# Polynomial convolution and attention in one launch: the first image in seven chunks of 448 pixels, its way out behind the next chunk's products, and scores copied with turned sign and a running minimum

## The chip, the cores and the metric

The kernel runs on one core of one Trainium2 chip. A core has TensorE (PE, matrix products; its weight loads are shown as PEld), VectorE (DVE), ScalarE (ACT), GpSimd (POOL) and SyncE (SP), which run side by side, each through its own list of instructions in order, and wait for each other by semaphores. SBUF is the on-chip memory of 128 partitions; PSUM holds what PE writes. DMAs are issued here by SP and, in the opening, by ACT.

The metric is the device time of one launch in microseconds (us). Before the change the median of three runs is 5033.5 us (5032.83 to 5038.3).

## What is computed

32 images of 64 channels and 56 x 56 pixels (3136) go through two layers, all in float32. Layer 0 multiplies channels of a group with each other, in pairs and triples, and takes weighted sums of these products. Layer 1 is attention of every pixel over every pixel, with a double softmax, then a 3x3 convolution per channel.

```python
# layer 0: 8 groups of 8 channels
p2 = x[:, :, _I2] * x[:, :, _J2]
y2 = jnp.einsum('bgihw,goi->bgohw', p2, W2).reshape(B, Ch, H, Wd) + b2[None, :, None, None]
p3 = x[:, :, _I3] * x[:, :, _J3] * x[:, :, _K3]
y3 = jnp.einsum('bgihw,goi->bgohw', p3, W3).reshape(B, Ch, H, Wd) + b3[None, :, None, None]
return inp + y2 * beta2 + y3 * beta3 * CONV3_SCALE
# layer 1
g = jnp.clip(_bn(conv1x1(l, w_inside), gamma1, beta1, mean1, var1), 0.0, 6.0)
theta = l[:, :c_red]                       # 32 of the 64 channels
f = jnp.einsum('niab,nicd->nabcd', theta, theta)
f = jax.nn.softmax(f.reshape(n, h * w, h, w), axis=1)
f = jax.nn.softmax(f.reshape(n, h * w, h * w), axis=2)
out = jnp.einsum('nabcd,nicd->niab', f.reshape(n, h, w, h, w), g) / h * w
out = depthwise_conv3x3(out, w_dw)
return _bn(out, gamma2, beta2, mean2, var2) + l
```

The products of the pixels' scores are symmetric, so the first softmax (over the key's axis) can be taken along rows of a tile of scores, and the second along the other axis by normalising sums.

## The kernel before

**Images and tiles.** Images are taken in pairs, 16 pairs, which share the 128 partitions of `y` (three buffers, `ys`). For each image the 3136 x 3136 scores are made in tiles of 128 pixels by 3136; a pair has 49 tiles (the two remainders of 64 pixels share one), 784 in all. Tile t goes through `scores` (PE writes half a tile of 1568 columns into the four banks `ps`, DVE copies it into `e`, twice), `first_softmax`, `second_softmax` (one exponential each on ACT, in place), and three tiles later (`LAG`) through `attend`, where PE multiplies it with g into the banks `av` and `ax`. The banks of `ps` exist once: the second half's scores wait for the first half's copy. There are four buffers of `e`.

**The statistics of a tile.** Each copy is a multiplication by 1.0 with a running maximum, whose result goes into one of two columns of `mx`. `first_softmax` takes the negative of the larger one with a `tensor_reduce` into `nm` (line 512 and following), and the exponential uses it as bias with scale 1.0. `second_softmax` takes the reciprocal `rz` of the sum `z`.

**Layer 0.** `x` lies in memory so that a tile of 128 partitions and w pixels of "0", "a", "2", "4" or "b" holds the channels rotated by some offset, once for each half k of an image's channels. `products` makes, for each k, the product q = x0 * xa, then p = q * x for "0", "2", "4" and "b", and p4 from the two tiles "c". `poly` multiplies rounds of these with weights on PE into a bank, and `poly_out` adds bias and input into `y` on DVE. A chunk has 242 pixels (`PCH`, 13 chunks, `PCS`), because in the steady stage its sum shares the bank `ax` with attention. Loads stand in a list `plan`; `prefetch` issues from it while a slot of the kind is free (`XB`: 7, 13 and 3 slots) and `credit` lasts, and `products` frees slots. Product buffers are counted by `ROOM` and `taken`.

**The order of the work.** Every engine's instructions are pinned to the order in which the program writes them (`Pinned`), DMAs too. Each DMA adds to one of eight counters, and one that takes up a counter waits until the earlier DMA on it has landed. The image that the first tiles need (image 0 of pair 0, channel halves `ONE`) is made ahead of the tile loop, under the key -1: `feed(0, c, ONE, dve)` puts all 13 chunks on the list, its loads alternately on SP and ACT and its products on DVE. `first_poly(c)` runs the 12 matmuls of chunk c, taking up products as they come, and then its `poly_out`; `first_g(c - 1)` follows with g for the pixels then ready: `g_in` on PE, `g_out` and `prepare` on DVE. After the last chunk `load_theta(0)` copies channels of `y` into four groups of partitions of `th` with four DMAs on SP, and the last g follows.

ACT's list begins with 15 loads of weights and constants, then the two square roots of the batch norms, then its share of the image's loads. DVE's list has the scaling of weights and the batch norms' constants ahead of the first product.

**The tile loop.** In each step t: `run(t, "loads")`, `run(t, "feed")`, a `pace` that renews `credit`, scores of half 0, attention of tile t - 3, units of layer 0 or of g (`aux0`, `aux1`), scores of half 1, and the exponentials. Image 1 of pair 0 (`TWO`) is put on the list at t = 0, its products made on POOL, its sums spread over the first tiles; the following pairs are made the same way, all four channel halves at once, in the tiles of the pair before.

Of the kernel before, what the change touches and what calls it, by code (L numbers as in the profile page):

```python
# [12 lines left out]
AX = mybir.AxisListType  # L13
# [57 lines left out]
def tile_poly_conv_attention(  # L71
# [123 lines left out]

    b3row = const.tile([128, C], FP, name="b3row")
# [13 lines left out]
    dve.tensor_tensor(bias0, bias0, t0, ALU.add)  # L210

# [9 lines left out]
    for k in range(GM):  # L221
# [13 lines left out]
    yt = yp.tile([128, 3, N], FP, name="y")  # L235
    ys = [yt[:, p, :] for p in range(3)]
    pool.memset(ys[0][C:, :], 0.0)
# [4 lines left out]

    LOADS = {
        "0": [(0, 1, 0, 0)],
        "a": [(0, 1, 0, 1)],
        "2": [(0, 1, 2, 0)],
        "4": [(0, 1, 4, 0)],
        "b": [(0, 2, 5, 0), (1, 2, 1, 0)],  # L250
    }
# [11 lines left out]
    def start(out, in_, queue=sync):  # L263
        credit[0] -= 1
        queue.dma_start(out=out, in_=in_)

    def load_next():
        tag, key = plan.pop(0)
        n, c, ks, name, k, queue = key
# [3 lines left out]
        if name == "c":  # L273
            t = xp.tile([128, 2, PCH], FP, name=f"xc_{ident}", tag=tag, bufs=XB[tag])
            at = slice(ks[0] * 32, ks[-1] * 32 + 32)
            for d in range(2):
                src = bass.AP(
                    x.tensor,
                    ((4 * n + ks[0]) * EXT + 4 * d) * 4 * N + p0,
                    [[EXT * 4 * N, len(ks)], [N, 32], [1, w]],  # L280
                )
                start(t[at, d, :w], src, queue)
            loaded[key[:-1]] = [t[at, d, :w] for d in range(2)]
            return
        t = xp.tile([128, PCH], FP, name=f"x{name}_{ident}", tag=tag, bufs=XB[tag])
        for s0, every, d, grow in LOADS[name]:
# [5 lines left out]
            start(t[s0::every, :w] if every > 1 else t[:, :w], src, queue)  # L292
        loaded[key[:-1]] = t[:, :w]
# [9 lines left out]
    def products(n, c, ks, eng):  # L303
# [16 lines left out]
        for k in ks:  # L320
# [4 lines left out]
            eng.tensor_tensor(q, x0[k], xa, ALU.mult)  # L325
# [3 lines left out]
        for r, of in enumerate(("0", "2", "4", "b")):  # L329
            rounds.append({})  # L330
            yield "pr", len(ks)
            for k in ks:
# [4 lines left out]
                eng.tensor_tensor(p, rounds[0][k], xr, ALU.mult)  # L337
# [8 lines left out]
        eng.tensor_tensor(p4, both[0], both[1], ALU.mult)  # L346
# [27 lines left out]
    def feed(n, c, ks, eng):  # L374
# [3 lines left out]
        for tag, name, k in todo:  # L378

            queue = act if eng is dve and len(plan) % 2 else sync  # L380
            plan.append((tag, (n, c, ks, name, k, queue)))
        feeds.append((products(n, c, ks, eng), None))
# [12 lines left out]
    def poly(n, c, ks, rs, acc=None):  # L395

# [3 lines left out]
        own = acc is not None  # L402
        if not own:
            acc = ax[:, AUX:]
        at = slice(ks[0] * 32, ks[-1] * 32 + 32)
        for r in rs:
            for k in ks:
                pe.matmul(
                    out=acc[k * 32 : k * 32 + 32, :w],
                    lhsT=wq[:, r, k % 2, :] if r < NRND else w4[at, k * 32 : k * 32 + 32],  # L410
                    rhs=rounds[r][k],
                    start=own and r == 0,
# [5 lines left out]
    def poly_out(n, c, ks, acc=None):  # L418

        if acc is None:  # L420
            acc = ax[:, AUX:]
# [6 lines left out]
            ys[n % 3][at, p0 : p0 + w], acc[at, :w], bias0[at], xc, ALU.add, ALU.add  # L428
# [5 lines left out]
    def load_theta(b):  # L434
        y = ys[b // 2 % 3]
        p0 = (b % 2) * C
        th = thp.tile([128, N], FP, name=f"th_{b}", tag=f"th{b % 2}")
        for r in range(4):
            start(th[r * 32 : r * 32 + 32, :], y[p0 : p0 + CRED, :])
        ths[b] = th  # L440
# [36 lines left out]
    def scores(t, half):  # L477
        n, kind, q = tile_at(t)
        if half == 0:
            es[t] = ep.tile([128, N], FP, name=f"e_{t}", tag="e")  # L480
            mx = sp.tile([128, 2], FP, name=f"mx_{t}", tag="mx")
            nm = sp.tile([128, 1], FP, name=f"nm_{t}", tag="nm")
            z = sp.tile([128, 1], FP, name=f"z_{t}", tag="z")
            rz = sp.tile([128, 1], FP, name=f"rz_{t}", tag="rz")
            stats[t] = mx, nm, z, rz
        p = ps.tile([128, HALF, BANK], FP, name=f"ps_{t}_{half}", tag="ps")
        for j in range(HALF):
# [12 lines left out]
        e = es[t][:, half * HALF * CH : (half + 1) * HALF * CH]  # L500
        dve.tensor_scalar(
            e.rearrange("p (j c) -> p j c", c=CH), p[:, :, :CH], 1.0, None, ALU.mult, ALU.max,
            accum_out=stats[t][0][:, half : half + 1],
        )

    def first_softmax(t):
        mx, nm, z, _ = stats[t]
        dve.tensor_reduce(nm, mx, AX.X, ALU.max, negate=True)
        act.activation(es[t], es[t], AF.Exp, bias=nm, scale=1.0, accum_out=z)

    def second_softmax(t):
        _, _, z, rz = stats.pop(t)
# [178 lines left out]
    put(-1, "aux0", lambda: [feed(0, c, ONE, dve) for c in range(NPC)])  # L691
    put(-1, "aux0", lambda: prepare(FOR_G))
    banks = {}

# [241 lines left out]
```

## Time and profile before

| What | Value |
|---|---|
| median of three runs | 5033.5 us |
| the profiled execution, whole | 5033.6 us |
| its span | 5031.8 us |
| granted PE clock, mean | 0.983 |
| start of the first copy of scores / first exponential | 146.92 us / 152.55 us |
| POOL's first product of image 1 | 146.20 us |
| exponentials, two for each tile | 2912 and 2896 ns |
| copy of half a tile of scores | 1790 ns |

The span is the time from the first to the last instruction of the profiled execution; the run's time has 1.8 us around it. Times within a profile count from the span's start. A row of instructions names the line, the engine and the operation, what it writes and reads, its shapes and count, the busy time and mean duration, and the idle time of the engine just before it with what ended that. All instructions pass through one helper, so they carry its line, L109, and are told apart by the tiles' names. The chain of waits is followed back from the last instruction to what released each step.

### The profile page before, as it was taken

What the parts mean: (1) busy time and instruction counts of PE and PEld (TensorE: products, weight loads), DVE (VectorE), ACT (ScalarE), POOL (GpSimd) and SP (SyncE); (2) the same over time, 40 slices, a digit from 0 to 9 for tenths busy, and PEclk for the clock granted to TensorE, in tenths of its full rate; (3) what the DMA queues carried; (4) which work ended last, traced back from release to release, by engine and by line L of the source; (5) the groups of instructions that cost most, each with busy time, mean ns of one, the idle gap of its engine ahead of it and who ended that gap; (6) DMA issues with size and microseconds to landing.
All of it is one profiled execution on the core that took longest, in us unless ns stands there. A gap on an engine that the chain in (4) does not pass through costs nothing.

```text
span 5031.8 us, 240733 instructions
## 1 busy us (share of the span) xinstructions
PE 4753.8 (94%) x105924; PEld 3340.6 (66%) x105924; DVE 4222.6 (84%) x6962; ACT 4545.5 (90%) x2356; POOL 3194.2 (63%) x4325
## 2 busy tenths in 40 slices
PE   3898999999999999999999999999999999999995
PEld 1465676776767677676766767676676767667663
DVE  4465698898989889898988989898898989889887
ACT  0577899999999999999999999999999999999995
POOL 0667585876858587585857758586775858677000
PEclk7899999999999999999999999999999999999998
DMA  5555656555565555655565565556556555654201
GB/s 144 140 153 152 150 147 149 145 146 143 143 147 144 147 142 144 145 147 139 152 149 137 142 148 148 139 149 149 143 137 145 151 142 145 151 139 120 44 10 33
DMA packets 892956, 684.17 MB, mean 136 GB/s; under 512 B 291584, under 2 KB 877568, under 8 KB 887808
## 3 DMA queue, kind: packets, MB, share of 16 engines
q1 hardware_dynamic: 879368, 659.52, 51.4%
q8 instruction: 828, 13.57, 1.1%
q10 hardware_dynamic: 12536, 9.25, 0.7%
q14 instruction: 224, 1.84, 0.1%
HBM read 565.65 MB, written 25.69 MB: 118 GB/s over the span
## 4 chain that ended last, share of the span: by engine, by line
PE 71%; DVE 21%; DMA 4%; issue 2%; POOL 1%; SPq 1%; ACT 0%; ACTq 0%; POOLq 0%; DVEq 0%
PE av L109 30%; PE ps L109 24%; PE ax L109 16%; DVE e L109 15%; DVE y L109 3%; DMA xc_None<-in_x_dram 2%; DVE num L109 1%; DMA xa<-in_x_dram 1%; SPq L109 1%; POOL p L109 1%; DMA x<-in_x_dram 1%; DVE rd L109 0%; DVE nm L109 0%; POOL q L109 0%; DMA xb<-in_x_dram 0%
## 5 line engine op out<-in xcount | busy, mean ns | idle before, releaser
L109 DVE TENSOR_SCALAR_CACHE_REDUCE e<-ps 128x1568 f32<-128x1568 f32 x1568 | 2806.6, 1790 | 508.1 <-PE ps L109 462.9
L109 PEld LDWEIGHTS av<-gq,e 128*64 128x64 f32 x64512 | 2014.1, 138 | 864.7 <-issue 806.7
L109 ACT ACTIVATE e<-e,nm 128x3136 f32<-128x3136 f32 x784 | 2282.8, 2912 | 310.8 <-DVE rz L109 228.3
L109 POOL TENSOR_TENSOR p<-q,x 128x242 f32<-128x242 f32 (+1 forms) x2418 | 1781.1, 769 | 939.6 <-PE ax L109 843.0
L109 ACT ACTIVATE e<-e,rz 128x3136 f32<-128x3136 f32 x784 | 2270.3, 2896 | 0.0
L109 PE MATMUL av<-gq,e 128*64 128x65 f32 x64512 | 2227.2, 225 | 3.9 <-ACT e L109 3.2
L109 PE MATMUL ps<-th 32*128 32x392 f32 (+1 forms) x12800 | 1489.4, 541 | 109.7 <-DVE e L109 96.7
L109 PEld LDWEIGHTS ps<-th 32*128 32x128 f32 (+1 forms) x12800 | 491.3, 181 | 448.0 <-DVE e L109 368.4
L109 DVE SCALAR_TENSOR_TENSOR y<-tt,wdt,y 128x605 f32<-128x605 f32 (+4 forms) x720 | 742.4, 1032 | 6.7 <-DMA tt<-tr 5.3
L109 POOL TENSOR_TENSOR p<-q,xb 128x242 f32<-128x242 f32 x806 | 592.5, 762 | 230.6 <-PE ax L109 218.1
L109 POOL TENSOR_TENSOR q<-x,xa 128x242 f32<-128x242 f32 x806 | 561.5, 722 | 216.0 <-DMA xa<-in_x_dram 208.2
L109 PE MATMUL ax<-gq,e 128*64 128x65 f32 x12288 | 489.7, 222 | 0.0
L109 PE MATMUL ax<-p,wq 128*32 128x242 f32 (+1 forms) x6448 | 481.5, 373 | 1.5
L109 PEld LDWEIGHTS ax<-gq,e 128*64 128x64 f32 x12288 | 425.3, 138 | 0.0
L109 POOL TENSOR_SCALAR y<-y,bias 128x616 f32<-128x616 f32 (+1 forms) x80 | 162.8, 2036 | 147.5 <-PE ax L109 137.7
L109 PEld LDWEIGHTS ax<-p,wq 128*32 128x32 f32 x6448 | 178.9, 109 | 111.4 <-POOL p L109 18.8
L109 DVE SCALAR_TENSOR_TENSOR y<-ax,bias,xc_None 128x242 f32<-128x242 f32 (+3 forms) x208 | 97.1, 467 | 108.8 <-PE ax L109 103.1
L109 POOL TENSOR_TENSOR p<-xc_None 128x242 f32<-128x242 f32 (+3 forms) x208 | 127.6, 614 | 78.8 <-DMA xc_None<-in_x_dram 68.6
L109 PE MATMUL ax<-wit,y 128*64 128x64 f32 x3136 | 143.8, 223 | 18.6 <-DVE ax L109 9.6
L109 PE MATMUL ax<-p,w 128*32 128x242 f32 (+1 forms) x1612 | 123.9, 369 | 31.6 <-POOL p L109 31.6
L109 ACT ACTIVATION_READ_ACCUMULATOR e<-e,nm 128x1 f32 x784 | 145.6, 186 | 0.0
L109 DVE TENSOR_REDUCE nm<-mx 128x1 f32<-128x2 f32 x784 | 121.7, 155 | 27.2
(73 smaller groups left out, 1368.1 us busy)
## 6 DMA issues: line engine op xcount, KB each, us to landing
x<-in_x_dram SPq DMA_DIRECT2D x2268, 121.0 KB
xb<-in_x_dram SPq DMA_DIRECT2D x1512, 60.5 KB
xa<-in_x_dram SPq DMA_DIRECT2D x756, 121.0 KB
th<-y SPq DMA_DIRECT2D x128, 392.0 KB
xc_None<-in_x_dram SPq DMA_DIRECT2D x360, 121.0 KB
x<-in_x_dram SPq DMA_DIRECT2D x190, 116.0 KB
out_dram<-y SPq DMA_DIRECT2D x64, 308.0 KB
tt<-tr SPq DMA_DIRECT2D x128, 100.0 KB
```

What stands on the lines that cost most here:

```text
L109: i = f(*args, **kw)
```

## The change

Two parts are changed.

**The first image.** The 13 chunks of 242 pixels become seven of 448 (`FW`, `FCS`), each with a PSUM bank of its own: the four banks of `ps` and the three of `av`, which nobody else uses yet. Loads go into slots of 448 columns of the four buffers of `e` (28 slots, 12 for a chunk), products into slots of `ys[1]`, `ys[2]` and `tt` (21 slots, 10 for a chunk; p4 is written over its second input). Loads alternate between SP and ACT one by one. The loads of chunks 0 and 1 and the products of chunk 0 are written ahead of the scaling of weights; products of chunk 1 and loads of chunk 2 after it, ahead of the batch norms. Then for each chunk c: the matmuls of c, the sum of c - 1, the loads of c + 2, the products of c + 1, and g of c - 1. At c = 5 the first five chunks of theta are copied (2240 columns), and image 1's loads are put on the list, 12 of them issued at once; the other 896 columns follow after the last sum. Products of layer 0 in the tile loop stay on POOL, loads there on SP.

**The scores.** The copy multiplies by -1.0 and keeps a running minimum. The first half's minimum goes to column 0 of `nm`; the second half's copy takes that column as its second scalar, one value for each partition, and leaves the minimum of both in column 1. The `tensor_reduce` is gone, and the exponential has scale -1.0 and that column as bias.

```diff
+    FW = N // 7
+    FCS = [(p, FW) for p in range(0, N, FW)]
+    firsts = [ep.tile([128, N], FP, name=f"first_{i}", tag="e") for i in range(4)]
+    fx, fp = parts(firsts), parts(ys[1:] + [tt])
...
+    def first_loads(c):
+        p0, w = FCS[c]
+        def load(dst, k, d, grow, steps):
...
+            (act if fat["q"] % 2 else sync).dma_start(out=dst, in_=src)
+            fat["q"] += 1
...
+    def first_products(c):
+        xs = fxs[c]
...
+        q = {k: product(xs["0", k], xs["a", k]) for k in (0, 1)}
+        frs[c] = [q] + [{k: product(q[k], xs[a, k]) for k in (0, 1)} for a in "024b"]
+        dve.tensor_tensor(xs["c", 1], xs["c", 0], xs["c", 1], ALU.mult)
+        frs[c].append(dict.fromkeys((0, 1), xs["c", 1]))
+    first_loads(0)
+    first_loads(1)
+    first_products(0)
     b3row = const.tile([128, C], FP, name="b3row")
...
     dve.tensor_tensor(bias0, bias0, t0, ALU.add)
+    first_products(1)
+    first_loads(2)
     s1 = rsqrt_eps("bn1", row("var1"), C)
...
-            mx = sp.tile([128, 2], FP, name=f"mx_{t}", tag="mx")
-            nm = sp.tile([128, 1], FP, name=f"nm_{t}", tag="nm")
+            nm = sp.tile([128, 2], FP, name=f"nm_{t}", tag="nm")
...
         dve.tensor_scalar(
-            e.rearrange("p (j c) -> p j c", c=CH), p[:, :, :CH], 1.0, None, ALU.mult, ALU.max,
-            accum_out=stats[t][0][:, half : half + 1],
+            e.rearrange("p (j c) -> p j c", c=CH),
+            p[:, :, :CH],
+            -1.0,
+            nm[:, :1] if half else None,
+            ALU.mult,
+            ALU.min,
+            accum_out=nm[:, half : half + 1],
         )
     def first_softmax(t):
-        mx, nm, z, _ = stats[t]
-        dve.tensor_reduce(nm, mx, AX.X, ALU.max, negate=True)
-        act.activation(es[t], es[t], AF.Exp, bias=nm, scale=1.0, accum_out=z)
+        nm, z, _ = stats[t]
+        act.activation(es[t], es[t], AF.Exp, bias=nm[:, 1:], scale=-1.0, accum_out=z)
...
+    prepare(FOR_G)
+    NF = len(FCS)
+    first_poly(0)
+    for c in range(1, NF):
+        first_poly(c)
+        first_out(c - 1)
+        if c + 2 < NF:
+            first_loads(c + 2)
+        if c + 1 < NF:
+            first_products(c + 1)
+        if c == 5:
+            load_theta(0, 0, FCS[5][0])
+            for b in range(NPC):
+                feed(0, b, TWO)
+            credit[0] = 12
+            advance()
+        first_g(c - 1)
+    first_out(NF - 1)
+    load_theta(0, FCS[5][0], N)
+    first_g(NF - 1)
```

## The prediction

> **What bounds the kernel now.** I read the page's first two parts, then stretches of time one by one, because the two edits lie in different stages: one in the opening, one in every tile of scores.
>
> ```profile
> span 5031.8 us, 240733 instructions
> PE 4753.8 (94%) x105924; PEld 3340.6 (66%) x105924; DVE 4222.6 (84%) x6962; ACT 4545.5 (90%) x2356; POOL 3194.2 (63%) x4325
> ```
>
> The 94% is a mean. By stretches (columns: stretch, length, busy us and instructions of PE, PEld, DVE, ACT, POOL, then granted clock, DMA share, GB/s):
>
> ```profile
> 20.00:40.00 20.00, 5.33 (x24) 2.15 (x22) 10.63 (x31) 0.00 (x0) 0.00 (x0) 0.67 0.70 188
> 80.00:100.00 20.00, 8.94 (x72) 4.33 (x72) 11.23 (x34) 0.00 (x0) 0.00 (x0) 0.67 0.57 158
> 180.00:200.00 20.00, 16.82 (x288) 9.91 (x280) 9.14 (x16) 11.61 (x6) 15.01 (x24) 1.00 0.52 142
> 1000.00:1400.00 400.00, 395.07 (x9036) 281.32 (x9030) 355.79 (x578) 383.65 (x199) 288.07 (x388) 1.00 0.55 142
> ```
>
> There are three stages. In the **opening** (to the first exponential at 152.55) no engine is over 60% busy, and DMA is at 0.57 to 0.70. In the **second stage** (to some 280 us) POOL makes image 1's products beside the first tiles. In the **steady stage** PE is 98.8% busy. What sets the pace of the opening is in the chain of waits (start, us, what):
>
> ```profile
> 52.72 0.53 SPq L109
> 53.31 0.61 SPq L109
> 53.97 0.60 SPq L109
> 54.62 5.19 DMA xa<-in_x_dram
> 60.48 0.41 DVE p L109
> ```
>
> Three issues at 0.6 us, a landing of 5.19 us, one product, then again: a loop of latency. Buffers come free only as DVE consumes, and each load also waits until an earlier one has landed on its counter (eight, shared by the SP and ACT queues). A chunk's sum leaves PSUM at 52.24 and at 122.89, eight chunks apart: 8.8 us for 242 pixels. The last sum is at 134.76, theta is issued from 135.24, and its four parts reach PE at 139.28, 141.12, 143.10 and 145.21.
>
> In the second stage the chain repeats every 9.3 us: p4 products of POOL end a wait for the xc load at 156.15, 164.92, 174.31, 184.62 and so on to 241.21. In the steady stage the chain has two faces: PE alone (av, ax, ps), and where attention is light, a ring:
>
> ```profile
> 2612.98 1.81 DVE e L109 x2
> 2614.83 0.98 PE ps L109 x8
> 2615.84 1.81 DVE e L109 x2
> 2617.69 1.06 PE ps L109 x8
> ```
>
> There is one set of score banks, so scores wait for the copy and the copy for scores, 2.86 us a half. "DVE e" is 15.1% of the whole chain: 760 us / 1.81 = 420 of 1568 copies.
>
> **The opening, part by part.** Pixels and bytes stay: 7 chunks of eight loads of 229 KB, four of 115 and four of 57 make 2.52 MB a chunk, 17.7 MB in all. Issues fall from 13 x 14 = 182 to 7 x 16 = 112, on two queues at 0.6 us: 4.8 us a chunk, not a bound. Costs of a chunk of 448:
> - DVE: a 128x242 product takes 405 ns alone, six in a row 2.01 us, 335 each, so 83 beyond 242/0.96 ns. For 448: 467 + 83 = 550 ns, eleven make 6.05 us. With the sum (0.68) and one or two groups of g (0.4 to 0.7 each) 7.3 us.
> - DMA: 188 GB/s at a share of 0.70 is 268 at full share. I take 274, as packets are twice as long (1792 B; no row shows them): 9.2 us. The ends are 13.4 us (188 GB/s, the best 20 us seen) and DVE's 7.3 us.
> - PE: a chunk of 242 took 5.20 us in the chain at 123.40 and 2.65 at 129.43 (two chunks in 5.29). Times 448/242: 9.6 and 4.9 us.
>
> Two rules are weighed here. The Trainium skill ("DMA: Bandwidth & Descriptors", Bandwidth) says to batch transfers to a MiB, and that those under 64 KB are descriptor-dominated. Its table (0.95 us for 64 KB, 6.15 for 1 MB) gives about 1.84, 1.23 and 0.9 us for the three sizes, 23 us a chunk taken singly: 161 us, no gain at all. The row speaks otherwise: 121 KB would by that table take 1.26 us, 96 GB/s, and 20 to 40 us moved 188, so transfers overlap; I go by the row. The other ("TensorE: Matmul & The Clock Gate", Part 1) has PE at half clock until a window of about 3.4 us was busy. The rows agree (0.67; 5.20 against 2.65). By the cold price PE needs 9.6 us a chunk and ties with DMA; by the warm one it is hidden. Products now come in runs of 6 us, so I take mostly warm.
>
> The order written out: sum of c-1, loads of c+2, products of c+1, g of c-1. The sum has poly of c-1 finished a whole product run earlier, so PE's tail is covered by products; if PE is cold throughout that cover is gone, about 1 us a chunk. Loads have two chunks of lead, 15 us against a landing of 5, so latency is covered and only the rate remains.
>
> The times: ACT's queue holds the weight loads until 11.2 us, and SP's fourth load waits on a counter of theirs, as SP did here until 10.26. So from 12 us, with 0.69 MB already moved: chunks 0, 1, 2 land at 20.6, 29.8, 39.0. New wait: the square roots of batch norm now stand behind the ACT half of chunk 2's loads, to 35; DVE's chain behind them (13.46 to 18.68 here) ends at 41, and sum 0, products 2 and chunk 3's loads stand behind it. Sum 0 at 41.7, products 2 end 47.8, products 3 at 55.1, products 4 at 62.4. From there landing leads: chunk 5 lands 69.6, chunk 6 at 78.8. At chunk 5 SP also issues the first theta part (4 x 287 KB) and 12 loads for image 1: 2.3 MB behind chunk 6's loads, which I charge with 2 us. Products 6 end 81.4; poly's rest, sum 5 and g give sum 6 at 86.
>
> Then the way out: g groups 2.6 (134.76 to 137.4 here), scores 1.7 cold (148.77), copy 1.87, scores 1.7, copy 1.87, 0.3: first exponential at 96 instead of 152.55. The split theta pays here: its second part (4 x 115 KB, issued 86 to 88.6, landing near 91) lies behind g and the first half. Four more issues are its price, 2.6 us of SP.
>
> What is late next is POOL's loop. Its first xc load stands on SP behind theta: 86 + 2.6 + 1.2 of own issue + 3.5 = 93 against 156.15, **62 to 63 us earlier**. POOL's earlier products wait ready. Its period of 9.3 us and the tiles behind it are untouched, so the shift carries to the end. Tiles shift by 56.5 at least and follow POOL in this stage: I take 62.
>
> **The scores.** Removed per tile: one reduce. Added: a pointer scalar in the second copy.
>
> ```profile
> L109 DVE TENSOR_REDUCE nm<-mx 128x1 f32<-128x2 f32 x784 | 121.7, 155 | 27.2
> 2604.39 1.79 DVE L109 TENSOR_SCALAR_CACHE_REDUCE e<-ps 128x1568 f32<-128x1568 f32 x1 [0.30 <-PE ps L109]
> 2606.22 0.15 DVE L109 TENSOR_REDUCE nm<-mx 128x1 f32<-128x2 f32 x1
> 2606.30 0.15 DVE L109 RECIPROCAL rz<-z 128x1 f32<-128x1 f32 x1
> 18.28 0.23 DVE L109 TENSOR_SCALAR wdt<-wdt,r_bn 128x9 f32<-128x9 f32 x1
> ```
>
> 121.7 us of reduces go, but in the ring DVE waits for PE beside them, and in PE's stretches nobody waits. Only where "DVE nm" is on the chain does it pay: 0.2 to 0.3% of the chain in four stretches of 100 to 500 us, say 0.25%, 12.6 us or 81 tiles; the next instruction starts 0.08 after the reduce, so 6 to 12 us, taken as 9. The exponential may start 0.2 us earlier, but ACT waits for nobody behind it. The pointer: 0.23 us for nine elements against 0.15 for the 128x1 immediates, so up to 0.08; from below 0[...]. I take 0.065. It lies on the ring in 210 second copies: 13.6 us. The second copy's wait for the first one's accumulator is met a ring half earlier. Sign and minimum cost nothing else: same operation, one pass. Sum: +5 us.
>
> **Total.** The profiled execution took 5033.6, 1.8 beyond its span; the runs' median is 5033.5, so no correction. 5033.6 - 62 + 5 = 4976.6: **4977 us**. What this measurement can tell from no change is about 0.2%, 10 us.
>
> **The rivals.**
> - *The loads stay at 188 GB/s* (chance 0.15). For: the loops of before never did better over 20 us. Against: their waits were for buffers. Landings of chunk 6 then near 106, first exponential near 122 and gain 31: 5033.6 - 31 + 5 = 5008.
> - *The reduce was worth more* (0.08): tiles with DVE, ACT and PE all near their limit gain its whole length on one tile in three, 260 x 0.155 = 40 us, with no pointer price: 5033.6 - 62 - 40 = 4932. Against: PE's idle time from 600 to 4600 us is 66 us in all.
> - *The second copy is dearer* (0.05): pointer and minimum cost c more in every tile. On the ring 210c; past 0.3 us (the gap between PE's 6.0 and the ring's 5.72 us a tile) all 784 tiles pay. At c = 0.3 the 63 us eat the opening's gain, so it decides from there; at 0.4: 5034 - 62 + 63 + 78 = 5113. Against: no DVE row shows more than 0.08.
> - *The opening's gain is absorbed* (0.03): POOL's loop, or pair 1's products behind it, ends where it did: 5030. Against: POOL's start moves as well.
>
> The forecast itself (gain of 45 to 75 in the opening) has 0.69. Its own bounds: DVE-bound chunks and a free pointer give 5033.6 - 70 - 9 = 4955; a cold PE, 5 us later, and the full pointer price (17) about 4987. The range reaches up past the first rival and down a little: 4950 to 5010, leaving out most of the second and the third. Faster by over 0.2%: 0.92; within: 0.03; slower: 0.05.
>
> **What would show it.** First exponential near 96, last sum near 86; DMA at 230 GB/s or more from 45 to 80 us (188 means the first rival); sums 7 to 9 us apart; the first xc product of POOL near 93 and the following ones still 9.3 apart; second copies at 1.79 to 1.87 us against the first ones' 1.79; no reduce; PE busy as before after 600 us. I am wrong if the shift at the first exponential is not found again at the end of the second stage, or if the ring's period changes by more than 0.1 us.

## The result and the profile after

Four runs of the changed kernel gave a median of 4986.6 us (4981.65 to 4990.56), beside 5034.9 for the kernel before on the same chip. The ratio is 0.990 (95% interval 0.9886 to 0.9920). The forecast was 4977 us, range 4950 to 5010. The profiled execution, the fastest of the four, took 4981.65 us against 5033.6, 52 less; its span and engines:

```profile
span 4979.8 us, 239326 instructions
PE 4740.9 (95%) x105780; PEld 3327.3 (67%) x105780; DVE 4132.8 (83%) x6106; ACT 4552.8 (91%) x2356; POOL 3202.0 (64%) x4325
```

DVE has 90 us less to do and PE 13, so where the 52 us came from has to be read by stage. Two stretches of the opening before the change (columns as in the prediction), then three of it and the steady stretch after:

```profile
40.00:60.00 20.00, 9.97 (x60) 4.06 (x60) 9.97 (x28) 0.00 (x0) 0.00 (x0) 0.65 0.58 164
60.00:80.00 20.00, 10.50 (x84) 4.77 (x84) 10.40 (x31) 0.00 (x0) 0.00 (x0) 0.87 0.55 146
```

```profile
20.00:40.00 20.00, 11.23 (x48) 2.74 (x48) 12.82 (x40) 1.54 (x2) 0.00 (x0) 0.92 0.69 220
40.00:60.00 20.00, 15.44 (x85) 5.97 (x86) 17.93 (x46) 0.20 (x1) 0.00 (x0) 0.82 0.80 243
60.00:80.00 20.00, 17.44 (x81) 4.52 (x80) 16.71 (x33) 1.28 (x1) 0.00 (x0) 1.00 0.85 259
1000.00:1400.00 400.00, 391.43 (x8946) 279.07 (x8944) 343.37 (x502) 386.61 (x200) 268.28 (x362) 1.00 0.58 146
```

In the opening DMA moves 220 to 259 GB/s, not 146 to 188, PE's clock is 0.82 to 1.00 instead of 0.65 to 0.87, and DVE goes from 50 to 56% busy to 64, 90 and 84%. The steady stretch hardly differs. For the rest of this text I use the **lead**: how much earlier a tile's first exponential starts than in the profile of before.

| Tile | 0 | 8 | 26 | 60 | 98 | 735 | 783 |
|---|---|---|---|---|---|---|---|
| after | 53.4 | 55.9 | 59.5 | 56.8 | 56.8 | 55.9 | 53.3 |
| opening alone (first experiment) | 51.7 | 53.2 | 52.4 | 47.1 | 47.1 | 47.1 | 47.1 |
| scores alone (second) | 2.3 | 1.1 | 3.0 | 2.4 | 2.6 | 2.8 | 0.1 |
| neither pointer nor reduce (third) | 56.9 | 57.0 | 60.7 | 59.3 | 59.8 | 68.9 | 69.0 |
| issues shared by SP and ACT (eleventh) | 51.9 | 54.1 | 71.9 | 70.4 | 70.0 | 69.9 | 69.9 |

The gain is made before the first tile and lasts; 0.9 is lost between tiles 98 and 735 and 2.7 in the last pair.

A lead belongs to one execution. The second experiment has the opening of before and is still 2.3 ahead at tile 0; kernels with the new opening unchanged have their last sum at 86.9 (full change), 88.3 (first) and 83.7 (third). So differences of up to some 3 us in the opening can't be told from chance. The profiled execution of the first experiment was the slowest of its four (4986.1, median 4977.4). And the runs come from several chips, on which the median of the kernel before lies between 5026.5 and 5034.9 us; between experiments I therefore compare ratios to it, 0.001 being 5 us.

The times of DVE in the opening, from its timeline (start, duration, instruction, and in brackets the idle time before it and what ended it):

```profile
37.48 0.55 DVE L108 RECIPROCAL r_bn<-s_bn 128x64 f32<-128x64 f32 x1 [6.22 <-ACT s_bn L108]
42.68 0.67 DVE L108 SCALAR_TENSOR_TENSOR y<-first_s,bias,first 64x448 f32<-64x448 f32 x1
50.62 0.67 DVE L108 SCALAR_TENSOR_TENSOR y<-first_s,bias,first 64x448 f32<-64x448 f32 x1 [0.73 <-PE first_s L108]
...
86.92 0.67 DVE L108 SCALAR_TENSOR_TENSOR y<-first,bias,first 64x448 f32<-64x448 f32 x1
```

The foreseen wait for the square root is there: 6.22 us, because ACT issues its first 24 loads from 12.40 to 35.86 and only then turns to the table load and the root. The sums start at 42.68, 50.62, 58.56, 65.69, 76.39, 83.51 and 86.92: 7.1 to 7.9 us a chunk while DVE leads, 10.7 where the loads of chunk 5 are late (DVE waits 3.2 us for them).

The sums at 50.62 and 58.56 wait 0.7 us for PE, although the matmuls of their own chunks were done. For the first of them, PE's last matmuls of chunks 1 and 2:

```profile
33.55 0.94 PE L108 MATMUL first_s<-first,w 64*32 64x448 f32 x4
49.63 0.94 PE L108 MATMUL first_s<-first,w 64*32 64x448 f32 x4
```

The sum of chunk 1 starts when chunk 2's matmuls end (50.57), 16 us after its own. The banks of chunks 0 to 3 are one tile of the program, `first_s`, and the wait follows the tile: the sum of chunk 3, with no later matmul in that tile, and those after it, whose banks are tiles of their own, don't wait for PE.

Behind the opening, SP's own list (start, time until the group is issued, what, how many):

```profile
78.22 3.92 SPq L108 DMA_DIRECT2D th<-y  x4
82.18 1.39 SPq L108 DMA_DIRECT2D x<-in_x_dram  x1
...
91.39 2.48 SPq L108 DMA_DIRECT2D th<-y  x4
93.92 1.29 SPq L108 DMA_DIRECT2D xc_None<-in_x_dram  x2
```

Theta's second part needs sum 6, done at 87.6, but stands behind the twelve loads for image 1 and is issued at 91.39. Scores of the second half wait for it, the second copy waits for them, and the first exponential starts at 99.20 (152.55 before):

```profile
97.30 1.85 DVE L108 TENSOR_SCALAR_CACHE_REDUCE e<-ps,nm 128x1568 f32<-128x1568 f32 x1 [4.17 <-PE ps L108]
99.20 2.91 ACT L108 ACTIVATE e<-e,nm 128x3136 f32<-128x3136 f32 x1 [23.71 <-DVE e L108]
```

The first xc load follows theta, and POOL's loop starts there; its p4 products, first and last of image 1, before (L109) and after (L108):

```profile
156.15 0.61 POOL L109 TENSOR_TENSOR p<-xc_None 64x242 f32<-64x242 f32 x1 [2.62 <-DMA xc_None<-in_x_dram]
...
269.20 0.59 POOL L109 TENSOR_TENSOR p<-xc_None 64x232 f32<-64x232 f32 x1 [1.94 <-DMA xc_None<-in_x_dram]
```

```profile
99.57 0.61 POOL L108 TENSOR_TENSOR p<-xc_None 64x242 f32<-64x242 f32 x1 [5.18 <-DMA xc_None<-in_x_dram]
...
212.70 0.59 POOL L108 TENSOR_TENSOR p<-xc_None 64x232 f32<-64x232 f32 x1 [1.46 <-DMA xc_None<-in_x_dram]
```

56.6 us earlier at the first and 56.5 at the thirteenth: the loop keeps its 9.4 us a chunk and carries the shift. Last, the copies:

```profile
L108 DVE TENSOR_SCALAR_CACHE_REDUCE e<-ps 128x1568 f32<-128x1568 f32 x784 | 1403.7, 1790 | 325.9 <-PE ps L108 297.9
L108 DVE TENSOR_SCALAR_CACHE_REDUCE e<-ps,nm 128x1568 f32<-128x1568 f32 x784 | 1448.2, 1847 | 249.6 <-PE ps L108 246.7
```

The copy that takes a column as its second scalar is 57 ns longer (1847 against 1790), in the mean of all 784 tiles.

### The profile page after: what moved, and what is told of

Same layout as the page of the kernel before. It is cut to its first block, busy times and chain, and to the rows that moved or that the text cites. A ratio compares the mean times of both kernels' runs of the same rounds, so it can differ in the third digit from the quotient of the medians.

```text
span 4979.8 us, 239326 instructions
## 1 busy us (share of the span) xinstructions
PE 4740.9 (95%) x105780; PEld 3327.3 (67%) x105780; DVE 4132.8 (83%) x6106; ACT 4552.8 (91%) x2356; POOL 3202.0 (64%) x4325
## 3 DMA queue, kind: packets, MB, share of 16 engines
q1 hardware_dynamic: 874892, 659.46, 51.9%
## 4 chain that ended last, share of the span: by engine, by line
PE 78%; DVE 12%; DMA 3%; ACT 2%; issue 1%; POOL 1%; SPq 1%; ACTq 0%; POOLq 0%; DVEq 0%
PE av L108 34%; PE ps L108 26%; PE ax L108 18%; DVE e L108 10%; ACT e L108 2%; DMA xc_None<-in_x_dram 2%; DVE y L108 1%; POOL p L108 1%; DMA x<-in_x_dram 1%; SPq L108 1%; DVE num L108 1%; PE first_s L108 0%; DMA first<-in_x_dram 0%; DMA xa<-in_x_dram 0%; POOL q L108 0%
## 5 line engine op out<-in xcount | busy, mean ns | idle before, releaser
L108 PEld LDWEIGHTS av<-gq,e 128*64 128x64 f32 x64512 | 2010.1, 138 | 862.0 <-issue 854.8
L108 ACT ACTIVATE e<-e,nm 128x3136 f32<-128x3136 f32 x784 | 2283.1, 2912 | 298.5 <-DVE e L108 273.7
L108 POOL TENSOR_TENSOR p<-q,x 128x242 f32<-128x242 f32 (+1 forms) x2418 | 1817.2, 784 | 937.4 <-PE ax L108 925.4
L108 ACT ACTIVATE e<-e,rz 128x3136 f32<-128x3136 f32 x784 | 2270.4, 2896 | 0.0
L108 PE MATMUL av<-gq,e 128*64 128x65 f32 x64512 | 2223.6, 225 | 3.4 <-ACT e L108 3.0
L108 DVE TENSOR_SCALAR_CACHE_REDUCE e<-ps 128x1568 f32<-128x1568 f32 x784 | 1403.7, 1790 | 325.9 <-PE ps L108 297.9
L108 DVE TENSOR_SCALAR_CACHE_REDUCE e<-ps,nm 128x1568 f32<-128x1568 f32 x784 | 1448.2, 1847 | 249.6 <-PE ps L108 246.7
L108 PE MATMUL ps<-th 32*128 32x392 f32 (+1 forms) x12800 | 1488.1, 541 | 113.3 <-DVE e L108 104.2
L108 PEld LDWEIGHTS ps<-th 32*128 32x128 f32 (+1 forms) x12800 | 492.2, 181 | 450.4 <-DVE e L108 371.3
L108 DVE SCALAR_TENSOR_TENSOR y<-tt,wdt,y 128x605 f32<-128x605 f32 (+4 forms) x720 | 722.7, 1004 | 6.6 <-DMA tt<-tr 5.2
L108 POOL TENSOR_TENSOR p<-q,xb 128x242 f32<-128x242 f32 x806 | 570.1, 734 | 229.9 <-PE ax L108 221.2
L108 POOL TENSOR_TENSOR q<-x,xa 128x242 f32<-128x242 f32 x806 | 569.9, 733 | 153.9 <-DMA xa<-in_x_dram 148.7
L108 PE MATMUL ax<-gq,e 128*64 128x65 f32 x12288 | 489.4, 222 | 0.0
L108 PE MATMUL ax<-p,wq 128*32 128x242 f32 (+1 forms) x6448 | 483.5, 374 | 2.4 <-POOL p L108 0.8
L108 PEld LDWEIGHTS ax<-gq,e 128*64 128x64 f32 x12288 | 424.8, 138 | 0.0
L108 PEld LDWEIGHTS ax<-p,wq 128*32 128x32 f32 x6448 | 179.2, 109 | 113.4 <-POOL p L108 20.8
L108 POOL TENSOR_SCALAR y<-y,bias 128x616 f32<-128x616 f32 (+1 forms) x80 | 148.1, 1853 | 148.8 <-PE ax L108 148.8
L108 DVE SCALAR_TENSOR_TENSOR y<-ax,bias,xc_None 128x242 f32<-128x242 f32 (+3 forms) x208 | 97.1, 467 | 126.4 <-PE ax L108 126.3
L108 POOL TENSOR_TENSOR p<-xc_None 128x242 f32<-128x242 f32 (+3 forms) x208 | 127.5, 613 | 79.9 <-DMA xc_None<-in_x_dram 73.7
L108 PE MATMUL ax<-wit,y 128*64 128x64 f32 x3136 | 143.6, 223 | 13.1 <-issue 9.0
L108 PE MATMUL ax<-p,w 128*32 128x242 f32 (+1 forms) x1612 | 123.9, 370 | 31.4 <-POOL p L108 31.4
L108 ACT ACTIVATION_READ_ACCUMULATOR e<-e,nm 128x1 f32 x784 | 145.8, 186 | 0.0
```

The source lines that it names most:

```text
L108: i = f(*args, **kw)
```

## The experiments

**1 and 2: each part alone.** The first kernel has the new opening and the scores of before, the second the reverse.

```diff
-            -1.0,
-            nm[:, :1] if half else None,
-            ALU.mult,
-            ALU.min,
-            accum_out=nm[:, half : half + 1],
+            e.rearrange("p (j c) -> p j c", c=CH), p[:, :, :CH], 1.0, None, ALU.mult, ALU.max,
+            accum_out=stats[t][0][:, half : half + 1],
...
+        dve.tensor_reduce(nm, mx, AX.X, ALU.max, negate=True)
+        act.activation(es[t], es[t], AF.Exp, bias=nm, scale=1.0, accum_out=z)
```

> The new opening with the scores of before (factor 1.0, running maximum in two columns, tensor_reduce, scale 1.0). Theory A, the pointer scalar costs its 57 ns where the ring of scores and copy sets the pace and the reduce was nearly free: the lead over the kernel before stays at 56 to 57 us from the second stage to the end and does not fall in the last pair; time 3 to 5 us below the full change, near 4980 where the full change has 4984. Rival B, the removed reduce is worth tens of microseconds: 5000 to 5020, slower than the full change.

> The kernel before with the new scores alone (factor -1.0, running minimum, pointer scalar in the second copy, no reduce). Theory A: 3 to 5 us slower than before, 5037 to 5040, with all of it in the last pair of images (about 2.7 us) and in the ring stretches. Rival B: 5000 or less. If scores and opening add up, this difference and the one of the opening alone make the full change.

The opening alone took 4977.4 us (ratio 0.9887, interval 0.9871 to 0.9902); by the ratios that is 8 us below the full change, but the intervals overlap. The scores alone took 5034.3, ratio 1.0011 (1.0002 to 1.0019): by the ratio slower by some 5 us, between 1 and 10. That comes from five of its 13 runs (5040.6 to 5053.6 us); the other eight lie between 5032.8 and 5034.7, and the median is only 0.9 above that of before (5033.4). In the last pair, where nothing stands beside the scores, the difference is plain in the chain of waits. The full change, and then the opening alone (start, us, what):

```profile
4702.73 1.87 DVE e L108 x2
...
4705.66 1.81 DVE e L108 x2
...
4708.52 1.87 DVE e L108 x2
```

```profile
4702.27 1.81 DVE e L109 x2
...
4705.13 1.81 DVE e L109 x2
...
4707.99 1.81 DVE e L109 x2
```

From one copy of a kind to the next it is 5.79 us against 5.72. That is the ring of the prediction with the pointer in it: every second step is 1.87 long. The lead falls there by 2.7 in both kernels with the new scores, and by nothing in the other.

**3: neither pointer nor reduce.** The row's minimum is left out of the softmax (a constant bias takes its place), so that both prices are gone at once. The exponential then waits for no statistic either; what that alone is worth the run doesn't separate.

```diff
-            nm[:, :1] if half else None,
+            None,
...
-        act.activation(es[t], es[t], AF.Exp, bias=nm[:, 1:], scale=-1.0, accum_out=z)
+        act.activation(es[t], es[t], AF.Exp, bias=bias0, scale=-0.001, accum_out=z)
```

> The full change, but the second copy has no pointer scalar and the exponential takes a constant column as bias and scale -0.001; the row's minimum is left out of the softmax. It has neither reduce nor pointer. Theory A: both copies at 1.79 us, the lead does not fall in the last pair, 3 to 8 us below the full change and at most 4 below the opening alone (that difference is the reduce's price). Rival B: 30 us or more below the opening alone.

4968.4 us (ratio 0.9871, interval 0.9858 to 0.9885): by the ratios 16 us below the full change and 8 below the opening alone, whose interval it overlaps. The leads say where. Between tiles 98 and 735 this kernel, little by little, wins 9.0 us on before, which has the reduce (59.8 to 68.9); the opening alone, which has it too, wins nothing (47.1 to 47.1). So the **reduce is worth 9 us** on the path, with the wait for it. The full change loses 0.9 over the same tiles where this one wins 9.0, so the **pointer costs 9.9 us** there and 2.7 more in the last pair. By line, the chain from 700 to 4200 us of before and of after:

```profile
by line: PE av L109 34.8%; PE ps L109 26.4%; PE ax L109 18.8%; DVE e L109 13.8%; DVE y L109 2.5%; DVE num L109 1.6%; issue 0.6%; DVE rd L109 0.3%; DVE nm L109 0.3%; DVE ax L109 0.2%; DMA xb<-in_x_dram 0.1%; SPq L109 0.1%; DVE rz L109 0.1%; 
```

```profile
by line: PE av L108 39.4%; PE ps L108 28.7%; PE ax L108 20.9%; DVE e L108 9.2%; DVE num L108 0.7%; DVE y L108 0.5%; issue 0.4%; DVE rd L108 0.1%; DVE ax L108 0.1%; DVE rz L108 0.0%
```

"DVE nm" (0.3% of 3500 us, 10 us) is gone in the second, and "DVE e" falls from 13.8% to 9.2% (7.5% in the third kernel): an engine with less to do is less often the last to arrive, and the chain runs over PE instead. Shares move far more than time does; only the leads give the time.

**4: image 1 not ahead.** Its loads are put on the list at tile 0, as before, and SP's list behind chunk 6 holds theta only.

```diff
-            for b in range(NPC):
-                feed(0, b, TWO)
-            credit[0] = 12
-            advance()
...
+        if n == 0:
+            put(0, "feed", lambda: [feed(0, c, TWO) for c in range(NPC)])
```

> The full change, but image 1's loads go on the list at t = 0 as before; no 12 loads between the two parts of theta. Theory P, the second stage follows the loop of POOL and its xc loads: the second theta part is issued at about 88 instead of 91.4 and the first exponential comes at about 95.5 instead of 99.2, but the first xc product of POOL comes at about 106 instead of 99.6, tile 48 is 6 to 7 us later, and the time is 6 to 7 us above the full change. Rival, the tiles set the second stage: the time is 3 to 4 us below the full change.

4982.1 us (0.9901, interval 0.9886 to 0.9916), not to be told from the full change. Theta's second part was issued right behind the last sum, at 86.6, and the first exponential came 3.7 us earlier: 2.3 of it is the second copy's wait for scores (1.89 us instead of 4.17), so much the twelve loads had cost; the rest is an opening that was a microsecond earlier even before the edit takes effect (sum 4 at 75.34, not 76.39). POOL's first p4 came only 2.9 later (102.46), and by tile 48 the lead was 3.5 below the full change's. The twelve loads ahead are almost worthless: they cost the first tile about what they save the loop.

**5: ACT issues image 1's first chunk.** Its 14 loads go to ACT's queue, which has nothing to issue by then.

```diff
-        sync.dma_start(out=out, in_=in_)
+        queue[0].dma_start(out=out, in_=in_)
...
-            credit[0] = 12
+            credit[0] = 14
+            queue[0] = act
             advance()
+            queue[0] = sync
```

> The full change, but the first 14 loads of image 1 (the 12, and the two xc) are issued by ACT, whose queue is empty then, instead of SP. Theory P: the second theta part is no longer behind them and is issued at about 88, the first xc product of POOL comes at 90 to 93 instead of 99.6, the loop of 9.3 us follows it, and the time is 6 to 9 us below the full change. Rival, the tiles or the DMA rate set the second stage: at most 4 us below.

4982.1 us (0.9902, interval 0.9886 to 0.9919): no gain. The first p4 came at 87.44, 12 us earlier; the second came at 105.30, 3 us earlier. The first exponential was no earlier (99.22), because the last sum was 1.9 us later (88.86): DVE waited 2.0 us for chunk 6's loads, and POOL's products now ran beside DVE's. DVE's last product and six of POOL's, first in the full change, where they don't meet, then here, where they do:

```profile
82.33 0.61 DVE L108 TENSOR_TENSOR first<-first 64x448 f32<-64x448 f32 x1
89.11 3.97 POOL L108 TENSOR_TENSOR p<-q,x 128x242 f32<-128x242 f32 x6
```

```profile
84.00 1.11 DVE L108 TENSOR_TENSOR first<-first 64x448 f32<-64x448 f32 x1
78.35 6.28 POOL L108 TENSOR_TENSOR p<-q,x 128x242 f32<-128x242 f32 x6
```

Both slow down: a product of DVE from 0.61 to 1.11 us, six of POOL from 3.97 to 6.28. SP's list shows why the second p4 was late: after theta it issued chunk 1 from 92.01 on and took until 101.02 over it, in 0.55 to 0.65 us each, with no pause. Up to here I took the 9.4 us of the loop for the latency of loads waiting for slots. This run gave another theory: **SP's issuing itself is the pace**, 14 loads of about 0.64 us a chunk, and a chunk that comes early gains nothing for the ones behind it. SP's list in the full change, one whole chunk in the midst of the loop:

```profile
150.41 1.12 SPq L108 DMA_DIRECT2D xc_None<-in_x_dram  x2
151.59 0.56 SPq L108 DMA_DIRECT2D x<-in_x_dram  x1
152.25 0.56 SPq L108 DMA_DIRECT2D xa<-in_x_dram  x1
...
154.19 2.48 SPq L108 DMA_DIRECT2D x<-in_x_dram  x4
156.77 2.48 SPq L108 DMA_DIRECT2D xb<-in_x_dram  x4
159.34 1.11 SPq L108 DMA_DIRECT2D xc_None<-in_x_dram  x2
```

From one xc to the next 8.93 us, and between the groups nothing but 0.03 to 0.14 us. (Over the whole loop, 91 to 215 us, the profile has SP wait 47 times for slots that POOL frees, 1.2 us at most and 19.2 in all. Many of these waits lie within an issue of the usual 0.55 us and lengthen nothing, so 19.2 is too much; but part of the 9.4 us is this.) A queue with no gaps is a busy engine, though the page counts none of its instructions as busy.

**6: theta in one part**, after the last sum.

```diff
-            load_theta(0, 0, FCS[5][0])
...
-    load_theta(0, FCS[5][0], N)
+    load_theta(0)
```

> The full change, but theta is copied in one piece of 392 KB for each of the four DMAs after the last sum. The twelve loads of image 1 come first on SP and end about 4 us earlier. Theory P: theta is issued at 87.6, its parts land about 2 us apart up to 98 or 99, the first exponential is at 102 to 104 (3 to 5 later), and the xc loads behind theta's issues come at about the same time as now, so POOL's loop and the total move by 0 to 3 us only. Rival, the first exponential carries through: 4 to 6 us above the full change.

4989.7 us (0.9916, interval 0.99 to 0.9932; runs from 4980.1 to 5001.0), which doesn't tell it from the full change. In the profile, of its fastest run, the first exponential was 3.6 us later and POOL's first p4 as early (99.12); at tile 8 the lead was 56.2, that of the full change. As far as the profile shows, the split of theta helps the first tile, and POOL's loop takes it back.

**7: each sum at once**, without a product run of the next chunk in front of it.

```diff
     first_poly(0)
+    first_out(0)
     for c in range(1, NF):
         first_poly(c)
-        first_out(c - 1)
+        first_out(c)
```

> The full change, but each chunk's sum is written right behind its own matmuls, ahead of the next chunk's products, so nothing covers PE's tail on DVE. If the cover is what the order brings: DVE waits 2 to 4 us for PE at every chunk, sums come 9.5 to 11 us apart instead of 7 to 8, the last sum comes 10 to 20 us later than 86.9, and the total is that much above the full change. Rival, loads set the pace of the opening: less than 5 us.

4979.2 us (0.9894, interval 0.9879 to 0.9909), no slower. Sums came 7.94 apart and the last at 88.20, 1.3 us later. This is a miss: I had expected 10 to 20 us. PE in the same stretch:

```profile
60.00:80.00 20.00, 18.38 (x89) 4.72 (x86) 18.01 (x36) 1.28 (x1) 0.00 (x0) 1.00 0.86 260
```

Two things are behind it. At a clock of 1.00 PE takes up products as DVE makes them and has one round left when DVE ends, so that most sums wait only 0.7 us. And what DVE waits for PE it need not wait for loads: after 25 us it waited 10.2 us for PE's sums (6.7 of them at chunk 1, whose matmuls in `first_s` stood behind sum 0) instead of 1.5, but 0.2 for loads instead of 3.9, and 4.3 for the square root instead of 6.2. "A chunk's way out behind the next one's products" is worth a microsecond or so here, with chunks this long, PE this warm, and loads that would be waited for otherwise.

**8: the batch norms' square roots ahead of the image's loads**, which takes away the 6.2 us wait of DVE.

```diff
+    s1 = rsqrt_eps("bn1", row("var1"), C)
...
     first_loads(0)
     first_loads(1)
```

> The full change, but the batch norms' constants (two square roots on ACT, 26 small DVE instructions) are written ahead of the first loads and products. If DVE's 6.2 us of waiting for ACT's square root at 31 us and the 5 us of constants behind it set the opening: sum 0 comes at about 31 to 33 instead of 42.7, and the last sum 5 to 10 us earlier, near 78 to 82. Rival, loads at 240 to 260 GB/s set it: the last sum moves by less than 4 us. The total moves with POOL's start in either case, by no more than half of that, since POOL's loads stand on SP behind chunk 6's.

4980.3 us (0.9901, interval 0.9887 to 0.9916). Sum 0 was 3 us earlier, the last one 0.9 (86.03), which is within chance. The loads between 40 and 60 us:

```profile
40.00:60.00 20.00, 18.05 (x92) 5.17 (x92) 17.48 (x34) 0.00 (x0) 0.00 (x0) 1.00 0.86 269
```

What DVE did sooner it waited for later: after 25 us its waits for loads rose from 3.9 to 6.9 us and those for PE's sums from 1.5 to 4.3. By an estimate from the rows, 17.7 MB at about 250 GB/s need 71 us. The edit has a price of its own, so it doesn't isolate the wait: ACT issues its first load of the image at 17.03 instead of 12.40, and between 12 and 80 us either kernel moved 16.4 to 16.5 MB.

**9: fourteen chunks of 224 pixels** in the same order of work.

```diff
-    FW = N // 7
+    FW = N // 14
...
-        if c == 5:
-            load_theta(0, 0, FCS[5][0])
+        if c == 11:
+            load_theta(0, 0, FCS[10][0])
```

The seven banks are taken in turn (`banks[c % 7]`).

> The full change with 14 chunks of 224 pixels in the same order, slots of 224 columns (56 and 42 of them), banks taken in turn. If long DMAs bring the gain (eight in flight at most, each 0.6 us of issue; half the bytes each): DMA at 150 to 200 GB/s instead of 243 to 259 between 40 and 80 us, the last sum at 105 to 115 instead of 86.9, total 15 to 25 us above the full change. Rival, the free slots and two chunks of lead bring it, not the width: the last sum within 8 us of 86.9.

5002.0 us (0.9943, interval 0.9926 to 0.996), by the ratios 20 slower than the full change. The last sum came at 107.83, 21 later, and the lead of 35 at tile 8 stayed 34. The windows:

```profile
40.00:60.00 20.00, 18.16 (x132) 8.13 (x128) 17.01 (x55) 0.00 (x0) 0.00 (x0) 0.93 0.67 185
60.00:80.00 20.00, 14.93 (x100) 6.76 (x98) 13.88 (x41) 0.00 (x0) 0.00 (x0) 0.91 0.75 206
```

With loads of half the size DMA moved 185 and 206 GB/s instead of 243 and 259. So of the change's lead of some 56 us, about 21 goes with the size of a chunk, and 35 with the rest of the new order (slots for two chunks ahead, banks for more than one chunk, and what else differs), whose parts were not tried one by one. DVE was 85% and 69% busy in these windows, so in the second it is the loads that are missing; what the doubled number of products and issues adds was not measured by itself.

**10: two chunks of image 1 on ACT's queue**, with the scores of before: if SP sets the pace, two chunks taken off it should move the third.

```diff
-            credit[0] = 12
+            credit[0] = 28
+            queue[0] = act
             advance()
+            queue[0] = sync
```

> The new opening with the scores of before (as in the opening alone), and image 1's first 28 loads (two chunks) issued by ACT ahead of its first exponential. Theory S, in the second stage SP's issues set the pace (14 loads of 0.55 to 0.65 us, 8.9 to 9.5 us a chunk, without a gap in SP's list): SP then begins with chunk 2, the third xc product of POOL comes at 104 to 108 instead of 118, and the time is 8 to 12 us below the opening alone (4977): 4965 to 4969. Rival, POOL's own work or the tiles take over: at most 4 us below.

4981.0 us (0.9904, interval 0.9889 to 0.9919), no gain. The first p4 came at 86.72, the third at 113.34 (opening alone: 119.70), and the thirteenth at 211.88 (217.72), with the loop at 9.85 from the third on. Even this start doesn't shorten what the loop takes per chunk, and most of it was gone at once. It had a price too: the first exponential came at 105.27 (opening alone: 100.85), its first copy having waited 7.7 us for scores. The profiled execution, the slowest of its four, lost a further 8 us of its lead between tiles 600 and 637, which I can't explain.

**11: the issues of every chunk shared**, again with the scores of before. ACT issues 4 of the 14 loads of each chunk of image 1, the last xb pair and the xc pair.

```diff
+        queue[0] = act if n == 0 and (name == "c" or (name, k) == ("b", 3)) else sync
```

> The new opening with the scores of before, and of image 1's 14 loads a chunk ACT issues four (one xb pair and the xc pair), SP ten, through all 13 chunks. Theory S: SP's issues fall to 6.2 us a chunk, POOL's own work of 7.3 us becomes the pace, POOL's xc products come 7.3 to 8 us apart instead of 9.4, and the second stage ends 15 to 20 us earlier: 4957 to 4962. Rival, ACT's exponentials stand behind its DMAs' waits for counters: the products stay 9 us or more apart and the time is not below 4975.

**4966.6 us** (0.9875, interval 0.986 to 0.989), by the ratios 14 us below the full change and 6 below the opening alone, whose interval it overlaps. On the same chip and with the same scores, the tenth experiment took 4981.0, 14 us more, and their leads at tile 98 are 70.0 and 57.1. SP's list in this kernel, one of the shorter chunks:

```profile
127.30 0.59 SPq L109 DMA_DIRECT2D x<-in_x_dram  x1
127.98 0.55 SPq L109 DMA_DIRECT2D xa<-in_x_dram  x1
...
129.95 2.65 SPq L109 DMA_DIRECT2D x<-in_x_dram  x4
132.70 1.66 SPq L109 DMA_DIRECT2D xb<-in_x_dram  x2
134.40 0.59 SPq L109 DMA_DIRECT2D x<-in_x_dram  x1
```

7.1 us instead of 8.93, and POOL's p4 products went from 9.4 apart to 7.7 to 8.0 for most chunks; the thirteenth stood at 192.17 (212.70). What POOL waited for between 80 and 215 us, in the full change and then here (us in all, times, longest):

```profile
POOL p L108 <- DMA xc_None<-in_x_dram: 23.8, 11, 5.2
```

```profile
POOL p L109 <- DMA xc_None<-in_x_dram: 3.0, 4, 1.4
```

The lead of 54 at tile 8 becomes 72 at tile 26, and 70 stays to the end.

A rival stays open. In the full change the chain of waits runs through this loop as a latency: POOL's product at 139.38 frees a slot, SP issues the loads behind it, the last xc from 141.00 on, this lands 4.84 us later, and POOL's p4 starts at 146.58. The edit moves the xc pair itself, so it takes four issues off SP and also takes xc out from behind loads that wait for slots. Both shorten the loop, and no run here separates them.

Here a rule of the Trainium skill ("DMA: Bandwidth & Descriptors", Issuing engines are not separate DMA queues) has to be read with the trace: issuing from several engines, it says, saves only the sequencer's time, "which is usually small relative to the DMA itself". The first half agrees, that time is all that was saved; but of small loads in a row 14 x 0.64 us are 9 us, more than POOL's own work of some 7.4 us a chunk, and then it is not small.

**12: both**, sharing as in 11 and all 14 loads of chunk 0 on ACT.

> As the shared issues (scores of before, four of 14 loads on ACT), and all 14 loads of image 1's first chunk on ACT as well, so that theta's second part does not stand behind them on SP. Theory S: the loop keeps its 7.7 us, starts 3 to 8 us earlier, and the time is 2 to 6 us below the shared issues (4966.6). Rival, POOL's own 7.3 us a chunk and the tiles have taken over: within 2 us of it.

```diff
+        queue[0] = act if n == 0 and (c == 0 or name == "c" or (name, k) == ("b", 3)) else sync
...
-            credit[0] = 12
+            credit[0] = 14
```

4968.2 us (0.988, interval 0.9864 to 0.9897), not to be told from 11, thirteenth p4 at 196.37. Here the start itself hardly came about: the first p4 was 1.7 us earlier (92.55) and the second 2.9 later, and the last sum of the first image came at 91.28 instead of 85.08. As in experiment 5, DVE waited for chunk 6's loads (1.3 us), and seven of its products took 1.11 us each beside POOL's. So this run doesn't show what a start would be worth; it shows that work on image 1 given ahead can hold up the image in front of it.

## The prediction, step by step

- **The bound of the opening** (latency, not rate): right, by experiment 9 for some 35 us of the gain, the other 21 being the size of the loads. The first rival, loads that stay at 188 GB/s, fell: 220, 243 and 259. The forecast of 274 was 13% and 6% above the last two. The table weighed against it is headed as measured with transfers issued from GpSimd, and taken singly they gave 161 us; the loads here come from SP and ACT, and the last products of the opening started at 82.3. (In its working the first chunk should land at 18.7 by its own rate, not 20.6; nothing later rests on it.)
- **DVE's chunk** of 7.3 us: measured 7.1 to 7.9. Last sum forecast at 86, measured 86.9. PE mostly warm: right (0.82 to 1.00). The order behind the next products was to hide PE's tail: for chunks 1 and 2 it did not, as their sums waited for the next chunk's matmuls in `first_s`, and by experiment 7 there was little to hide; with PE warm the tail is 0.7 us.
- **The square root's wait**: DVE's chain behind it was forecast to end at 41 and ended at 42.7, with 6.2 us of waiting in it. It was given no price of its own; by experiment 8 the last sum doesn't move with it, though that edit delays loads as well.
- **Theta and the first exponential**, forecast at 96, came at 99.2. The step that failed is "its second part (4 x 115 KB, issued 86 to 88.6...)". It was issued from 91.39, 5.4 us later: 1.6 because sum 6 starts 0.9 later and takes 0.7 itself (it ends at 87.6), and 3.8 because SP had the twelve loads of image 1 in front of it. I had charged those loads with 2 us of bandwidth and not with their time on the queue.
- **POOL's loop**, forecast to start at 93 and 62 us earlier, started at 99.57 and 56.6 earlier. Of the 6.3 us missing from 86 + 2.6 + 1.2 + 3.5, 5.4 are the same delay of theta, and 0.9 the landing, 4.4 us instead of 3.5. The time on SP's queue, put at nothing and measured at 3.8 us, is the mis-sized term of the sum. The mechanism, that the shift carries through the loop to the end, held: 56.6 at the first product, 56.5 at the thirteenth, 56.8 at tile 98.
- **What paces the loop** was put as its period being "untouched", without a cause. It is SP's list for the most part: a start given ahead came to nothing (4, 5, 10), four issues of fourteen moved to another queue raised the lead at tile 98 by 13 us (11 against 10). Whether by their number or by xc's place behind the others stays open.
- **The scores**: forecast +5 us, as -9 and +13.6. Measured in the leads -9.0 and +9.9 + 2.7 = +12.6, so +3.6; the second experiment says +2.2 by its own leads, +0.9 by its median and +1 to +10 by its ratio. That the reduce came out at 9.0 is luck, its range having been 6 to 12. The pointer was taken at 65 ns and measured 57. The second and third rivals (a reduce worth 40 us, a copy dearer by 0.3 us or more) fell in their sizes; the sign of the trade was right.
- **The total**: with 56.6 for 62 and 3.6 for 5, 5033.6 - 56.6 + 3.6 = 4980.6, beside 4981.65 in the profiled execution. The median of runs is 5 us above that. The runs of this one kernel spread over 9 us, and the leads at tile 60 of kernels with the same loop range from 54 to 59 (experiments 3 to 8), and 47 in the slowest run of the opening alone; which wait of the second stage varies I haven't found. For the same reason it stays open why the opening alone is 8 us better than the full change by the runs where the leads give 3.6 for the scores, and why its own profiled execution lost 5 us of lead between tiles 26 and 60.

The fourth rival, that the gain is absorbed, was wrong for this change as a whole, but it is what happened to the further starts given to POOL's loop (5 and 10).

## What to carry to other kernels

Before a transfer is moved ahead, read the issuing queue as an engine: list its issues with their start times, and count what stands in front of the one that somebody waits for. A queue without gaps can be the bound, even where loads are small and DMA is half idle (0.55 from 100 to 213 us); here an early start for the first chunk was lost, and a second queue for a part of every chunk gained. Where an instruction is removed at the price of a longer one, price both where each is on the path, not by their totals: 121.7 us of reduces were worth 9 us, and 57 ns on every second copy, 45 us in all, cost some 12. And give every PSUM bank that is read on its own a tile of its own: where four shared one, a sum waited for matmuls that it didn't need.

## What was not expected of the hardware

- A column of scalars, one for each partition, made a copy of 128 x 1568 float32 from PSUM 57 ns longer, 3%.
- Loads of up to 229 KB, issued from two queues and at most eight in flight, ran at up to 269 GB/s (experiment 8), those of half the size in the same order at 175 to 206 (experiment 9, stretches of 20 us from 20 to 80).
- Issuing one load took SP 0.55 to 0.65 us whether it moved 124 KB or half of that; 14 of them, 8.93 us, took longer than the products of a chunk (some 7.4 us on POOL).
- A product of DVE of 448 columns took 1.11 us beside products of POOL and 0.61 without; POOL's, of 242 columns, 1.07 to 1.09 and 0.69 to 0.70 (experiment 5).
